# ScalarE in program order in the dense attentions, and a regrouped layer-3 FFN, in an eight-block transformer kernel

## The chip, the core and the metric

The kernel runs on one NeuronCore of a Trainium2 chip, in one launch. The core has five engines, each with an instruction queue of its own that it works off in order: TensorE (PE; its weight loads, PEld, are listed apart), VectorE (DVE), ScalarE (ACT), GpSimd (POOL), and SyncE (SP), which issues most DMAs. They wait for one another by semaphores. The metric is the device time of the launch in microseconds (us), the median of several runs.

## What is computed

The input x has 4 sequences of 512 rows of 128 channels, all float32. Four layers follow, each a "macaron": half of an FFN, an attention, half of the same FFN again.

```python
x = x + 0.5 * ffn_l(layernorm(x))
x = x + attn_l(layernorm(x))
x = x + 0.5 * ffn_l(layernorm(x))
```

The blocks that the change touches:

- **Layer-1 FFN**: a causal attention with 16 heads of 8 channels over all 512 rows, then a layer norm with weights (ln1), a gate over 8 experts of which two count, the experts' 128x128 products summed by the gates, and a second layer norm with weights (ln2).
- **Layer-3 attention**: 16 heads of 8, not causal, rotary queries and keys, biases on q, k, v and on the output (bo).
- **Layer-3 FFN**: two inner layers, each:

```python
h = shift_token(x)                       # half of the channels one row later
q, k, v = split(h @ wqkv)                # 8 heads of 64
o = local_attention(rotary(l2norm(q) * qs), rotary(l2norm(k) * ks), v)   # window 64
x = x + o @ wo
h = shift_token(x)
h = (h - mean(h)) / sqrt(var(h) + 1e-5) * lg + lb
a, g = split(h @ w1 + b1)                # 2 x 341
x = x + (a * gelu(g)) @ w2 + b2
```

The other blocks (layer 0, the layer-1 and layer-2 attentions, the routed layer-2 FFN) are left as they are.

## The kernel before

Rows lie on the 128 partitions as 16 tiles; TB = 4 tiles make a sequence b. Python loops write out all instructions. A scheduler then places them on the engines by estimated times and dependencies, except those handed to keep_in_program_order: these keep their order on their engine. Before the change all matmuls and transposes of these blocks are so held (mm_in_order, transpose_in_order), and the layer-3 FFN's ACT instructions (act, act_copy). DVE and POOL are free, and so is ACT in the dense attentions.

**Dense attention** (dense_attention, used by the layer-1 FFN with a causal mask and by the layer-3 attention without one). A unit is (sequence b, j) with four heads; it has four steps n of two half steps each. In a half step, PE writes scores pk_at, writes products pq_at for the maxima five steps ahead (LEAD), ACT turns pk_at into PT by Exp (L778), the maxima nm are taken on DVE (L743 unmasked, L748 masked), and PE multiplies PT of the step before with the values (po_at). The banks in PSUM: one double bank for pk_at, two for pq_at, one for po_at, one ("m") for all else. Work for the next sequence hangs at places relative to its first step: prepare gives pairs (place, function); half steps are tenths .5. marked_keys (L676) makes four copies of the keys with head channels masked, two on ACT (L683), two on DVE (L685). After each half step, tick runs parts of "chains": lists of (gap, function), each part due gap ticks after the one before. The experts of the layer-1 FFN (l1_experts) are such a chain: statistics of y, affine(1) (y scaled on ACT at L223 by scaled_by_act, then two products with the weights on POOL, or on DVE for the last sequence), turn, gates, choice, eight products, statistics, affine(2), residual. The root in the statistics is some ten small POOL steps (L184 to L194).

**Layer-3 FFN** (l3_ffn). A unit is (inner layer l, sequence b), eight in all, with four steps each; a step n runs stages for several tiles at once: project(n), exponentials(n-4), to_features(n-2), weights(n-3), turn_weights(n-5), with_values(n-6), at places 0 to 5. Around them stand the unit's parts from a list of (function, step after the unit's first, place); a part runs just before the stage of its place. PSUM has three double banks "d" (p_qk, pt_qk, ps3, pt3 and pag take turns in them) and two single "m".

```python
parts = [
    (attended, 10, 2), (mean, 10, 4), (variance, 11, 0), (normed, 11, 4), (lambda u: hidden(u, 0), 12, 2),
    (lambda u: hidden(u, 1), 12, 3), (lambda u: hidden(u, 2), 12, 5), (close_unit, 13, 2),
    (lambda u: leave(units[u][1]) if units[u][0] else None, 13, 5),
]
```

attended multiplies with wo (pz), adds into z = yT (L1690) and makes h by a shift, half on ACT, half on DVE (L1548). mean subtracts the mean (L1699) and squares (sq). variance sums the squares (pvar), copies them to rs (L1711), takes the root on POOL (rs L194), and spreads it over a diagonal dg (L1714, DVE). normed multiplies by ones (pb) and applies the norm in two DVE steps (L1724, L1725). hidden(u, c) makes one of three chunks of the gated product: pag on PE, Gelu on ACT into ge, hh on DVE (L1738). Gelu and Exp are in different ACT tables, so each group of gelus has two table loads.

Of the kernel before, what the change touches and what calls it, by code (L numbers as in the profile page):

```python
# [103 lines left out]
def tile_macaron(ctx, tc, x_in, const_in, vec_in, w0_in, ws_in, ws3_in, w2f_in, w3_in, out):  # L104
# [104 lines left out]
    def scaled(dst, src, b, stats):  # L209

        mv, r = stats
        for t in range(b * TB, b * TB + TB):
            i = t - b * TB
            nc.vector.tensor_scalar(dst[:, t, :], src[:, t, :], mv[:, i, 0:1], r[:, i : i + 1], ALU.subtract, ALU.mult)  # L214

    def scaled_by_act(dst, src, b, stats):

        mv, r = stats
        m = keep.tile([P, TB], F32, tag="ln_m", name="ln_m", bufs=3)
        nc.vector.scalar_tensor_tensor(m, mv[:, :, 0], -1.0, r, ALU.mult, ALU.mult)  # L220
        for i in range(TB):
            t = b * TB + i
            nc.scalar.activation(dst[:, t, :], src[:, t, :], AF.Identity, scale=r[:, i : i + 1], bias=m[:, i : i + 1])  # L223

    def normalize(dst, src, b, pinned=False):
        scaled(dst, src, b, statistics(src, b, None, pinned))
# [1 line left out]
    def turn(b):  # L228

        pt = bank("m", "pt_y")  # L230
        for t in range(TB):
            transpose_in_order(pt[:, ts(t, P)], y[:, b * TB + t, :])
        nc.scalar.copy(yT[:, b, :], pt)  # L233

# [441 lines left out]
    def marked_keys(sb, src, bias):  # L676


        km = sb.tile([P, 4, S], F32, tag="km", name="km", bufs=2)
        for j in range(4):  # L680
            mj, bj = kmask[:, j : j + 1], bias[:, j : j + 1]
            if j % 2:
                nc.scalar.activation(km[:, j, :], src, AF.Identity, scale=mj, bias=bj)  # L683
# [28 lines left out]
    def dense_attention(sb, prepare, finish, wo, masked, tiles=None):  # L712

        vhs, nms = tiles or attention_tiles(sb)
        seqs, units = {}, [(b, j) for b in range(B) for j in range(4)]
        n_steps = TB * len(units)
        qxs, PTs, pos, later = {}, {}, {}, {}
# [55 lines left out]
        def weights(step, half, pk):  # L775
            q0 = step % TB * P if masked else 0
            PT = sb.tile([P, 2, S], F32, tag="PT", name="PT", bufs=4)
            nc.scalar.activation(PT[:, :, q0:], pk[:, :, q0:], AF.Exp, scale=SC8)  # L778
# [36 lines left out]
        def output(b):  # L815
            pt = bank("m", "pt_ao")
            for t in range(TB):
                transpose_in_order(pt[:, ts(t, P)], seqs[b]["ao"][:, t, :])
            aoT = sb.tile([P, S], F32, tag="oT", name="aoT")
            nc.scalar.copy(aoT, pt)  # L820
            seqs[b]["aoT"] = aoT

        def project(b):
# [21 lines left out]
        for n in range(-LEAD, n_steps + 5):  # L845
            for half in range(2):
                pk = scores(n, half) if 0 <= n < n_steps else None
                if n + LEAD < n_steps:
                    maxima(n + LEAD, 1 - half)
                if pk is not None:  # L850
                    weights(n, half, pk)
                if 1 <= n <= n_steps:
                    with_values(n - 1, half)
                    if half and n % TB == 0:
                        u = n // TB - 1
                        oTs[u] = sb.tile([P, S], F32, tag="oT", name="oT")
                        nc.scalar.copy(oTs[u], pos.pop(u))
# [4 lines left out]
        assert not later, later  # L862


    def l1_ffn(tag, xb, l1_tiles):

        with pool(tag) as sb, banks(tag + "ps", **MIX):
# [4 lines left out]
            def prepare(b, vh, seq):  # L872
                def norm():
                    seq["ready"] = take(b)
                    if not seq["ready"]:
                        seq["stats"] = statistics(x, b)

                def scale():
                    if not seq["ready"]:
                        scaled(y, x, b, seq.pop("stats"))  # L880

                def features():
                    if not seq["ready"]:
# [12 lines left out]

                def queries():
                    pq = bank("m", "pq1")
                    mm_in_order(pq, WS(ws, "1f_wq"), seq["in"])
                    seq["q"] = sb.tile([P, S], F32, tag="qT", name="qT", bufs=2)  # L900
                    nc.scalar.activation(seq["q"], pq, AF.Identity, bias=bq)

                def keys():
                    pk = bank("m", "pk1")
                    mm_in_order(pk, WS(ws, "1f_wk"), seq["in"])
                    kT = sb.tile([P, S], F32, tag="kT", name="kT")
                    nc.scalar.copy(kT, pk)
# [14 lines left out]
    def l1_experts(sb, b):  # L922
# [15 lines left out]
        def gates():  # L938
# [8 lines left out]
            nc.scalar.activation(g, g, AF.Exp)  # L947

        def choice():
            g, r = st["g"], st["r"]  # L950
# [10 lines left out]
        def turn_gates():  # L961
# [4 lines left out]
            nc.scalar.copy(st["gT"], pt[:8, :])  # L966

        def biases():
            pb = bank("m", "pb")
# [41 lines left out]

        spare = chain(b)
        spare(2, statistics_of_y, False)
        spare(2, lambda: affine(1), False)
        spare(4, lambda: turn(b))
        alone = b == B - 1 and routed
        if alone:
# [14 lines left out]
            else:  # L1032
                spare(2, lambda t=t: both(t))
        spare(1, statistics_of_y, False)
        spare(2, lambda: affine(2), False)
        spare(2, residual, False)
        leave_normed(b, spare, 2)

# [441 lines left out]
    def l3_attn():  # L1480
        with pool("l3a") as sb:
            with banks("l3apa", **MIX):

                def prepare(b, vh, seq):
# [6 lines left out]
                    def second(n):  # L1491
# [2 lines left out]
                        t2 = sb.tile([P, S], F32, tag="t2", name="t2", bufs=2)  # L1494
                        nc.vector.scalar_tensor_tensor(t2, p2, WS3(ws3, f"3a_b{n}s"), ST, ALU.add, ALU.mult)
                        nc.gpsimd.tensor_add(seq[n], seq[n], t2)
                        if n == "k":
                            seq["k"] = marked_keys(sb, seq["k"], kmax)

                    return (  # L1500
                        (-14, lambda: begin_sequence(b)), (-13.5, lambda: first("k")), (-12, lambda: second("k")),
                        (-10.5, lambda: first("q")), (-9, lambda: second("q")),
                        (-7.5 if b else -4, lambda: values(vh, b, WS3(ws3, "3a_v"), VEC(vec, "3a_bv"))),
                    )

                def finish(b, pr):
                    xb = x[:, ts(b, TB), :]
                    nc.vector.tensor_add(xb, pr, xb)
                    nc.gpsimd.tensor_add(xb, xb, rows(VEC(vec, "3a_bo"), TB))
                    leave_normed(b, chain(b), 3)  # L1510

                dense_attention(sb, prepare, finish, WS3(ws3, "3a_o"), False)
# [9 lines left out]
    def l3_ffn(w3, tag, first):  # L1522
        with pool(tag) as sb, banks(tag + "ps", d=3, m=2):
# [180 lines left out]
            def variance(u):  # L1704
# [5 lines left out]
                rs = sb.tile([P, TB], F32, tag="rs", name="rs", bufs=2)  # L1710
                nc.vector.tensor_copy(rs, pv[:, : 2 * TB].rearrange("p (t i) -> p t i", i=2)[:, :, 0])  # L1711
                inverse_root(sb, rs, rs, "ir4", ALU.add, 1e-5, nc.gpsimd)
                dg = tmp("dg")
                nc.vector.scalar_tensor_tensor(  # L1714
                    dg.rearrange("p (t n) -> p t n", n=P), rows(ident, TB), float(D), bcast(rs, P), ALU.mult, ALU.mult
# [3 lines left out]
            def normed(u):  # L1719
# [1 line left out]
                h2 = u_state[u]["h2"]  # L1721
                pb = bank("m", "pb3")
                mm_in_order(pb, onesm, u_state[u].pop("dg"))
                nc.vector.tensor_mul(h2, h2, pb)  # L1724
                nc.vector.tensor_scalar(h2, h2, W(l, "lg"), W(l, "lb"), ALU.mult, ALU.add)  # L1725

            def hidden(u, c):
                l, b = units[u]
# [35 lines left out]
            if first:  # L1764
                for l in range(2):
                    tab = W(l, "tab").rearrange("p (t n) -> p t n", t=TB)
                    nc.vector.tensor_mul(tab, tab, rows(VEC(vec, f"3f_s{l}"), TB))

            parts = [
                (attended, 10, 2), (mean, 10, 4), (variance, 11, 0), (normed, 11, 4), (lambda u: hidden(u, 0), 12, 2),  # L1770
                (lambda u: hidden(u, 1), 12, 3), (lambda u: hidden(u, 2), 12, 5), (close_unit, 13, 2),
                (lambda u: leave(units[u][1]) if units[u][0] else None, 13, 5),
            ]
            later = {}
            for u in range(len(units)):
# [192 lines left out]
```

## Time and profile before

| | us |
|---|---|
| median of 3 runs | 2975.86 (2975.21 to 2979.55) |
| the profiled execution | 2971.15 |
| its span, first to last instruction | 2969.5 |
| busy: PE, DVE, ACT, POOL | 2266.3, 1828.9, 1242.9, 908.0 |
| layer-1 FFNs, from the first to the last Exp | some 450 to 760 and 940 to 1255 |
| layer-3 FFNs, first to last projection | 1681 to 2028 and 2531 to 2872 |
| layer-3 attention, first to last Exp | 2164 to 2515 |

Page and trace come from one execution, with times from the span's start. A busy share is an average over stages with different limits, so the views by window count most. In the list of waits, a line names the engine and line that waited, what released it, the total, how often, and the longest. The chain that ended last follows the end back through whatever released each step:

```profile
PE 49%; DVE 24%; ACT 11%; POOL 10%; issue 6%; DMA 1%; DVEq 0%; POOLq 0%; ACTq 0%; SPq 0%
```

### The profile page before, as it was taken

To read this page: it belongs to the slowest core of one execution; us is meant where nothing else is said; L and a number is where in the kernel's file an instruction comes from. 1 tells how busy PE (TensorE), PEld (TensorE's weight loads), DVE (VectorE), ACT (ScalarE), POOL (GpSimd) and SP (SyncE) were. 2 spreads that over 40 slices of the span, in tenths; PEclk is the share of its full clock that TensorE was granted. 3 is DMA by queue.
4 is the path that set the end of the run, shared out by engine and by line. 5 is a ranking of instruction groups with operands and counts; after the bars stand their busy time and mean duration, and the time that the engine had idled before them with its cause. 6 is when DMAs were issued, how large, how long until landed. Compare 5 with 4: busy or idle time off the path is not lost.

```text
span 2969.5 us, 46865 instructions
## 1 busy us (share of the span) xinstructions
PE 2266.3 (76%) x17534; PEld 1171.2 (39%) x17534; DVE 1828.9 (62%) x4796; ACT 1242.9 (42%) x2682; POOL 908.0 (31%) x1668
## 2 busy tenths in 40 slices
PE   4377439888678898849668578888688898688987
PEld 2145113333333333338358355555322222455553
DVE  4656476666576576554654587776455554787773
ACT  3054304433332433314323276666134344476663
POOL 1022012232122222212412486664100000777651
PEclk8588759999787999969768799998789999899998
DMA  3042010000000000017007210000000000110000
GB/s 132 0 154 76 0 58 1 1 1 1 1 1 1 1 1 4 5 57 257 15 16 263 72 26 19 21 19 9 0 1 1 1 1 1 26 24 18 23 19 11
DMA packets 33771, 99.12 MB, mean 33 GB/s; under 512 B 6184, under 2 KB 12072, under 8 KB 33032
## 3 DMA queue, kind: packets, MB, share of 16 engines
q1 hardware_dynamic: 30616, 88.03, 9.1%
q0 software_dynamic: 2496, 5.12, 0.8%
q8 instruction: 138, 2.26, 0.3%
q10 hardware_dynamic: 432, 2.98, 0.3%
q14 instruction: 89, 0.73, 0.1%
HBM read 66.88 MB, written 14.55 MB: 27 GB/s over the span
## 4 chain that ended last, share of the span: by engine, by line
PE 49%; DVE 24%; ACT 11%; POOL 10%; issue 6%; DMA 1%; DVEq 0%; POOLq 0%; ACTq 0%; SPq 0%
PE pk_at L164 10%; PE po_at L164 6%; ACT PT L778 4%; PE pa L164 3%; PE po L164 3%; PE pe L164 3%; PE pag L164 2%; PE pv L164 2%; DVE y L987 2%; PE pz L164 2%; PE pt L161 2%; PE pg L164 2%; POOL t L1591 2%; ACT s L1536 2%; DVE order L357 1%
## 5 line engine op out<-in xcount | busy, mean ns | idle before, releaser
L778 ACT ACTIVATE PT<-pk_at 128x1024 f32<-128x1024 f32 (+3 forms) x384 | 311.1, 810 | 535.0 <-PE pq_at L164 461.8
L164 PE MATMUL pk_at<-qx,km 32*128 32x512 f32 (+3 forms) x1536 | 370.6, 559 | 87.4 <-ACT PT L778 85.0
L164 PE MATMUL po_at<-PT,vh 128*32 128x512 f32 (+3 forms) x1536 | 335.8, 519 | 0.3 <-ACT PT L778 0.2
L748 DVE CUSTOM_DVE_ANT_0 s<-pq_at,cst 128x384 f32<-128x384 f32 (+3 forms) x512 | 248.5, 485 | 97.2 <-PE pq_at L164 85.4
L1536 ACT ACTIVATE s<-s,nm,rn 128x128 f32<-128x128 f32 x512 | 245.6, 485 | 14.2 <-DVE nm L1642 14.0
L781 POOL TENSOR_SCALAR_AFFINE_SELECT PT<-PT 128x256 f32<-128x256 f32 x256 | 106.9, 419 | 439.1 <-ACT PT L778 439.0
L164 PEld LDWEIGHTS pk_at<-qx,km 32*128 32x128 f32 x1536 | 121.1, 192 | 298.4 <-ACT PT L778 240.1
L164 PE MATMUL pq_at<-km,qT 32*128 32x384 f32 (+3 forms) x1024 | 223.9, 526 | 13.5 <-DVE nm L748 7.7
L743 DVE TENSOR_REDUCE nm<-pq_at 128x2 f32<-128x1024 f32 x128 | 156.4, 1225 | 115.1 <-PE pq_at L164 115.0
L1591 POOL TENSOR_TENSOR t<-t,t 128x1024 f32<-128x1024 f32 x64 | 151.3, 2364 | 152.7 <-DVE t L1587 149.9
L161 PE MATMUL pt_y<-ident,y 128*128 128x128 f32 x224 | 54.3, 369 | 166.2 <-DVE y L214 94.5
L164 PE MATMUL pq_at<-km,t 32*128 32x512 f32 x512 | 152.0, 700 | 5.0 <-DVE nm L743 2.8
L233 ACT COPY yT<-pt_y 128x512 f32<-128x512 f32 x56 | 32.8, 586 | 272.8 <-PE pt_y L161 272.8
L164 PE MATMUL p_qk<-w,hT 128*128 128x512 f32 x256 | 136.4, 658 | 13.2 <-DVE t L1587 9.1
L164 PEld LDWEIGHTS po_at<-PT,vh 128*32 128x32 f32 x1536 | 55.9, 109 | 218.1 <-issue 153.8
L1654 POOL TENSOR_TENSOR s<-s,sm 128x1024 f32<-128x1024 f32 x64 | 121.8, 1904 | 50.9 <-DVE sm L1653 46.0
L1536 ACT ACTIVATE sq<-p_qk 128x1024 f32<-128x1024 f32 x64 | 65.6, 1025 | 136.0 <-PE p_qk L164 90.1
L161 PE MATMUL pt<-ident,s 128*128 128x128 f32 x640 | 96.2, 299 | 33.9 <-POOL s L1654 14.3
L1584 DVE TENSOR_TENSOR t<-p_qk,w 128x1024 f32<-128x1024 f32 x64 | 78.2, 1221 | 60.9 <-ACT sq L1536 60.5
L161 PEld LDWEIGHTS pt_y<-ident,y 128*128 128x128 f32 x224 | 33.5, 168 | 199.3 <-issue 119.7
L164 PE MATMUL pag<-h,w 128*128 128x512 f32 (+1 forms) x192 | 101.7, 662 | 11.3 <-DVE h L1725 10.1
L161 PEld LDWEIGHTS pt<-ident,s 128*128 128x128 f32 x640 | 80.1, 154 | 69.3 <-issue 43.5
(421 smaller groups left out, 5149.3 us busy)
## 6 DMA issues: line engine op xcount, KB each, us to landing
w<-in_w2f_dram SPq DMA_DIRECT2D x46, 836.0 KB, 6.7
vb<-v SPq DMA_DIRECT2D x112, 128.0 KB, 2.2
skew<-qe SPq DMA_DIRECT2D x16, 512.0 KB, 3.0
rel<-skew SPq DMA_DIRECT2D x64, 128.0 KB, 3.4
w<-in_w_dram SPq DMA_DIRECT2D x1, 4147.0 KB, 12.6
w<-in_w_dram SPq DMA_DIRECT2D x1, 3200.0 KB
od<-o SPq DMA_DIRECT2D x46, 64.0 KB, 5.0
yd<-y SPq DMA_DIRECT2D x8, 256.0 KB, 2.3
```

The lines of the kernel that those rows point to most:

```text
L161: return nc.tensor.transpose(dst, src, ident[: src.shape[0], : src.shape[0]])
L164: tc.keep_in_program_order(nc.tensor.matmul(dst, lhsT=lhsT, rhs=rhs, start=start, stop=stop))
L233: nc.scalar.copy(yT[:, b, :], pt)
L743: nc.vector.tensor_reduce(to, pq.rearrange("p (i n) -> p i n", i=2), AX.X, ALU.max)
L748: nc.vector.tensor_tensor_reduce(s[:, :nk], pq[:, i * 512 : i * 512 + nk], causal[:, S - nk :], 1.0, -BIG, ALU.add, ALU.max, nm[:, qt, at ...
L778: nc.scalar.activation(PT[:, :, q0:], pk[:, :, q0:], AF.Exp, scale=SC8)
L781: nc.gpsimd.affine_select(d, d, pattern=[[0, 2], [1, P]], base=0, channel_multiplier=-1, compare_op=ALU.is_ge, fill=0.0)
L987: nc.vector.scalar_tensor_tensor(yt, pe[e // 4][:, ts(e % 4, D)], st["g"][:, t, e : e + 1], yt, ALU.mult, ALU.add)
L1536: tc.keep_in_program_order(nc.scalar.activation(*args, **kw))
L1584: nc.vector.tensor_mul(by_head(t1), by_head(p3), over(tab[:, 0]))
L1591: nc.gpsimd.tensor_add(t1, t1, t2)
L1654: nc.gpsimd.tensor_mul(s, s, bcast(sm, P))
```

## The change

1. A switch, ordered["act"], is on while a dense attention is written out; by_order then holds ACT's instructions in program order: PT, oT, aoT, qT, kT, the two ACT keys, yT, g, gT and the norm's y.
2. scaled_by_act makes m = -mean * r by two POOL steps instead of one DVE step. affine(1) and affine(2) of the experts come four ticks after the statistics instead of two.
3. Layer-3 attention: the keys are marked by a function of its own at place -11, not at the end of second("k") at -12; the output bias bo is added to x there, not after the projection.
4. Layer-3 FFN: exponentials and to_features change places, so that qT is copied before the exponentials; spread (dg) is a part of its own, half a step after variance; normed is one DVE step with lg, while lb goes through w1 into b1, once at the start (pn); the parts get other places, with hidden 0 at the end of one step and hidden 1 and 2 at the start of the next.

```diff
+    ordered = {"act": False}
+    def by_order(i):
+        if ordered["act"]:
+            tc.keep_in_program_order(i)
     def scaled_by_act(dst, src, b, stats):
-        nc.vector.scalar_tensor_tensor(m, mv[:, :, 0], -1.0, r, ALU.mult, ALU.mult)
+        nc.gpsimd.tensor_mul(m, mv[:, :, 0], r)
+        nc.gpsimd.tensor_scalar_mul(m, m, -1.0)
...
-            nc.scalar.activation(dst[:, t, :], src[:, t, :], AF.Identity, scale=r[:, i : i + 1], bias=m[:, i : i + 1])
+            by_order(nc.scalar.activation(dst[:, t, :], src[:, t, :], AF.Identity, scale=r[:, i : i + 1], bias=m[:, i : i + 1]))
...
-            nc.scalar.activation(PT[:, :, q0:], pk[:, :, q0:], AF.Exp, scale=SC8)
+            by_order(nc.scalar.activation(PT[:, :, q0:], pk[:, :, q0:], AF.Exp, scale=SC8))
...
-        spare(2, lambda: affine(1), False)
+        spare(4, lambda: affine(1), False)
...
-        spare(2, lambda: affine(2), False)
+        spare(4, lambda: affine(2), False)
...
                         nc.gpsimd.tensor_add(seq[n], seq[n], t2)
-                        if n == "k":
-                            seq["k"] = marked_keys(sb, seq["k"], kmax)
+                    def mark():
+                        seq["k"] = marked_keys(sb, seq["k"], kmax)
+                        xb = x[:, ts(b, TB), :]
+                        nc.gpsimd.tensor_add(xb, xb, rows(VEC(vec, "3a_bo"), TB))
...
-                        (-10.5, lambda: first("q")), (-9, lambda: second("q")),
+                        (-11, mark), (-10.5, lambda: first("q")), (-9, lambda: second("q")),
...
                     nc.vector.tensor_add(xb, pr, xb)
-                    nc.gpsimd.tensor_add(xb, xb, rows(VEC(vec, "3a_bo"), TB))
...
                 inverse_root(sb, rs, rs, "ir4", ALU.add, 1e-5, nc.gpsimd)
+                u_state[u]["rs"] = rs
+            def spread(u):
+                rs = u_state[u].pop("rs")
                 dg = tmp("dg")
...
                 mm_in_order(pb, onesm, u_state[u].pop("dg"))
-                nc.vector.tensor_mul(h2, h2, pb)
-                nc.vector.tensor_scalar(h2, h2, W(l, "lg"), W(l, "lb"), ALU.mult, ALU.add)
+                nc.vector.scalar_tensor_tensor(h2, h2, W(l, "lg"), pb, ALU.mult, ALU.mult)
...
+                    pn = bank("m", "pn")
+                    w1, a = W(l, "w1"), W3.at[f"lg{l}"][0]
+                    for half, name in ((0, "b1a"), (1, "b1g")):
+                        for c, (at, n) in enumerate(HCH):
+                            i = 2 * (3 * half + c)
+                            mm_in_order(pn[:n, i : i + 2], w1[:, half * HID + at : half * HID + at + n], w3[:, a : a + 2])
+                            to = W(l, name)[:n, c : c + 1]
+                            nc.vector.tensor_add(to, to, pn[:n, i + 1 : i + 2])
...
-                (attended, 10, 2), (mean, 10, 4), (variance, 11, 0), (normed, 11, 4), (lambda u: hidden(u, 0), 12, 2),
-                (lambda u: hidden(u, 1), 12, 3), (lambda u: hidden(u, 2), 12, 5), (close_unit, 13, 2),
-                (lambda u: leave(units[u][1]) if units[u][0] else None, 13, 5),
+                (attended, 10, 2), (mean, 10, 4), (variance, 11, 0), (spread, 11, 4), (normed, 12, 0),
+                (lambda u: hidden(u, 0), 12, 5), (lambda u: hidden(u, 1), 13, 0), (lambda u: hidden(u, 2), 13, 0),
+                (close_unit, 13, 4), (lambda u: leave(units[u][1]) if units[u][0] else None, 14, 0),
...
-                    (project, 0), (exponentials, 4), (to_features, 2), (weights, 3), (turn_weights, 5), (with_values, 6)
+                    (project, 0), (to_features, 2), (exponentials, 4), (weights, 3), (turn_weights, 5), (with_values, 6)
```

More of the change, by code (lines that the diff above doesn't have):

```diff
@@ L232, in turn @@
             transpose_in_order(pt[:, ts(t, P)], y[:, b * TB + t, :])
-        nc.scalar.copy(yT[:, b, :], pt)
+        by_order(nc.scalar.copy(yT[:, b, :], pt))
     clock, chains = [0], []
@@ L682, in marked_keys @@
             if j % 2:
-                nc.scalar.activation(km[:, j, :], src, AF.Identity, scale=mj, bias=bj)
+                by_order(nc.scalar.activation(km[:, j, :], src, AF.Identity, scale=mj, bias=bj))
             else:
@@ L716, in dense_attention @@
         vhs, nms = tiles or attention_tiles(sb)
+        ordered["act"] = True
         seqs, units = {}, [(b, j) for b in range(B) for j in range(4)]
@@ L819, in output @@
             aoT = sb.tile([P, S], F32, tag="oT", name="aoT")
-            nc.scalar.copy(aoT, pt)
+            by_order(nc.scalar.copy(aoT, pt))
             seqs[b]["aoT"] = aoT
@@ L856, in dense_attention @@
                         oTs[u] = sb.tile([P, S], F32, tag="oT", name="oT")
-                        nc.scalar.copy(oTs[u], pos.pop(u))
+                        by_order(nc.scalar.copy(oTs[u], pos.pop(u)))
                 fs = later.pop((n, half), ())
@@ L862, in dense_attention @@
         assert not later, later
+        ordered["act"] = False
     def l1_ffn(tag, xb, l1_tiles):
@@ L900, in queries @@
                     seq["q"] = sb.tile([P, S], F32, tag="qT", name="qT", bufs=2)
-                    nc.scalar.activation(seq["q"], pq, AF.Identity, bias=bq)
+                    by_order(nc.scalar.activation(seq["q"], pq, AF.Identity, bias=bq))
                 def keys():
@@ L906, in keys @@
                     kT = sb.tile([P, S], F32, tag="kT", name="kT")
-                    nc.scalar.copy(kT, pk)
+                    by_order(nc.scalar.copy(kT, pk))
                     seq["k"] = marked_keys(sb, kT, bkm)
@@ L946, in gates @@
             nc.vector.tensor_sub(g, g, bcast(r, 8))
-            nc.scalar.activation(g, g, AF.Exp)
+            by_order(nc.scalar.activation(g, g, AF.Exp))
         def choice():
@@ L965, in turn_gates @@
             st["gT"] = sb.tile([8, S], F32, tag="gT", name="gT")
-            nc.scalar.copy(st["gT"], pt[:8, :])
+            by_order(nc.scalar.copy(st["gT"], pt[:8, :]))
         def biases():
```

## The prediction

> **What bounds the kernel now.** I read the page first. TensorE (PE) is busy 76% of the 2969.5 us span and has 49% of the chain that ended last; VectorE (DVE) has 24%. No engine is full, so the next view is the busy time by stage: the first layer-1 FFN, the layer-3 attention, and the first layer-3 FFN up to its last projection. Columns: window and length, busy us of PE, weight load, DVE, ACT (ScalarE), POOL (GpSimd), granted clock, DMA share, GB/s.
>
> ```profile
> 450.00:760.00 310.00, 275.30 (x1804) 105.71 (x1804) 195.75 (x777) 119.14 (x189) 83.43 (x193) 0.93 0.00 1
> 2165.00:2520.00 355.00, 317.40 (x1712) 85.01 (x1712) 190.35 (x248) 146.67 (x157) 11.39 (x9) 0.97 0.00 1
> 1722.00:2027.00 305.00, 265.07 (x2380) 160.16 (x2381) 233.99 (x341) 206.17 (x552) 214.30 (x419) 0.96 0.09 20
> ```
>
> PE is close to full in all three and idles 35 to 40 us in each. Who makes it wait? The waits of these windows, in the same order (waiting engine and line, what it waits for: us, times, longest):
>
> ```profile
> ACT y L223 <- DVE ln_m L220: 12.5, 3, 5.0
> ...
> DVE ln_m L220 <- POOL ln_r L194: 8.5, 3, 3.4
> ...
> ACT km L683 <- POOL t L1496: 15.6, 3, 6.2
> ...
> DVE dg L1714 <- POOL rs L194: 22.1, 5, 4.5
> ...
> DVE hh L1738 <- ACT ge L1536: 14.8, 10, 1.9
> ...
> PE ps L164 <- DVE hh L1738: 13.2, 5, 2.6
> ```
>
> Each is one instruction at the head of an engine's queue. While ACT holds y or km, the exponentials PT (L778) behind it cannot free the score bank pk_at, which has one buffer, and PE stops. The timeline shows it in the layer-3 attention (start, length, engine; idle time before it in brackets); windows around two such gaps show the granted clock, the number after POOL's:
>
> ```profile
> 2282.42 1.52 ACT L683 ACTIVATE km<-t,cst 128x512 f32<-128x512 f32 x2 [6.24 <-POOL t L1496]
> ...
> 2284.90 1.22 PE L164 MATMUL pk_at<-qx,km 32*128 32x512 f32 x2 [5.75 <-ACT PT L778]
> ...
> 2190.30:2192.80 2.50, 0.00 (x0) 0.00 (x0) 2.13 (x3) 2.43 (x4) 0.04 (x1) 1.00 0.00 0
> 2193.00:2196.40 3.40, 3.40 (x12) 0.47 (x12) 1.23 (x1) 1.29 (x2) 0.00 (x0) 0.50 0.02 5
> ...
> 2284.90:2288.60 3.70, 3.70 (x12) 0.70 (x12) 1.23 (x1) 1.45 (x2) 0.00 (x0) 0.51 0.00 0
> ```
>
> PE does nothing for 5.75 us, and then its pairs take 1.22 us where they took 0.70: the gap costs twice.
>
> **Layer-1 FFNs: ScalarE in program order, ln_m on GpSimd.** PE idles 3.27, 4.50 and 4.76 us before pk_at in the first and 3.24, 4.50 and 3.17 in the second, 23.4 us together. Each time ACT holds y (L223), which waits for ln_m on DVE, which waits for POOL's root (ln_r). In the order that the changed program has on the engines, y stands three to five half steps later (behind the second 256-wide PT instead of the first 1024 or 384), and ln_m is on POOL directly behind its root. A unit of eight half steps took 14.5 to 17 us where nothing was added, so three are 6 us, more than the longest wait of 5.0. Both waits go, DVE's too. What is late next: y x4 (4x0.41), kT (0.58) and two km (1.5) now stand in a row on ACT, 3.7 us where the half step covers some 2.2: about 1.5 us of PE idle remains at four of the six places, 6 us. Clock: half speed followed the gaps for 3.4, 6.8 and 13.7 us in the first FFN, at most 12 us lost; the rows behind have other waits too, so I take 3.5 for each FFN. Sum: -(23.4 - 6) - 7 = **-24**; ends -10 and -40.
>
> Here a rule speaks against the edit: the Trainium skill (GPSIMD Engine Reference, 4.1 Engine selection) sends elementwise work to VectorE, since GpSimd takes about twice as long with two inputs. Row: ln_m takes 0.16 us on DVE, POOL's 128x4 product 0.20 and its scalar step 0.19. Two POOL steps for one on DVE cost 0.23 us more by the row, 0.48 if 0.16 is doubled for both: 16 times, 3.7 or 7.7 us of POOL. POOL is 27% busy here and covers either; only the last chain of the second FFN (some 1254 to 1300 us) lies bare, **+1**. I take the row; the edit's worth is the wait, not the duration. The experts' chains get four ticks longer and spill further into the layer-1 attention, where PE, DVE and ACT wait by turns: 0 to +4, taken as **+2**.
>
> **Layer-3 attention.** The keys' mark moves one step later, and x+bo (1.26 us on POOL) leaves the end of a sequence. ACT's 15.6 us of waiting for POOL's t go; PE idled 2.59, 5.75 and 5.75 us for them. But DVE isn't held to program order: in the changed order its two km still stand directly behind t (L1495) and ahead of nm. So DVE waits as before: t, POOL 1.27, km 1.0, then nm. The product bank pq_at has two buffers, so PE runs one half step on and stops at the next: nm ends at about 2284.3, pq_at is wanted at 2281.9, 2.4 us idle, at two places. Gain: 2x(5.75-2.4) + 2.6 = 9.3, and slow clock. There rule and row differ: the Trainium skill (TensorE: Matmul & The Clock Gate, Part 1) halves the clock after an idle window of about 3.4 us, which clears gaps of 2.4; in the rows above 2.59 us of idle was followed by 3.4 us at 0.50. By the rule all slow time goes (17 us, 8.5 saved), by the row only that at the first place (1.7). I stay near the row, 3.2: **-12.5**; ends -5 and -20. The four x+bo stand in the FFN before, ahead of POOL's root in its last steps: 1.3 on a chain there once or twice, **+2**.
>
> **Layer-3 FFNs.** DVE issues L1584 once a step. In one unit of four steps the starts lie 15.0 (attended, mean), 7.6, 17.2 (the gated products) and 9.7 us apart; by the starts of sq the mean of ten full units is 49.1. The third of them in the timeline:
>
> ```profile
> 1890.32 1.28 ACT L1536 ACT_TABLE_LOAD   x1
> ...
> 1892.20 0.58 ACT L1539 COPY qT<-pt_qk 128x512 f32<-128x512 f32 x1
> ...
> 1893.14 1.99 PE L164 MATMUL ps<-kT,qT 64*64 64x128 f32 x32 [2.64 <-DVE hh L1738]
> ```
>
> qT stands behind the exponentials, a table load and a gelu, and PE waits. DVE's work in a plain step, by its rows: 1.22 + 2x0.68 + 1.21 + kT 0.67 + s 1.22 + 0.20 + nm 1.21 + 0.29 + oT 0.68 = 8.05. The new steps, from start to start of L1584:
> - attended: z stands behind kT (4.5) and ends at 5.1 (pz is done at 4.0: p_qk 1.92, pv 0.86, pt_qk 0.87, pz 3.45, less 3.1 from p_qk's start to L1584's); ACT's h ends at 5.8. The exponentials now stand behind h, where they ran beside pz before: 3.9 us, to 9.7; sm 9.9, POOL's s to 11.8, root 2.9 to 14.7, dg 0.7: **15.4**. For dg still stands directly behind rs on DVE: spreading the variance in the source moves nothing there.
> - next: 8.05 and the one normed step, 0.75 (price of L1738, for 0.68 and 0.54): **8.8**.
> - gated: s frees pag's bank at 5.7, two products 3.4, p_qk 1.95, sq 1.0: **12.1**. qT is ahead, and nothing on PE waits for a gelu.
> - close: 8.05 + z 0.74 + hT 0.98: **9.8**.
>
> Together 46.1 for 49.1; ten units give -30. A half unit before each drain gives -1.5 more; in the drains nothing runs beside h, +2.5, less 0.5 for normed and 0.5 for the gelus: these cancel. **-30**; ends -61 and +5. The 2-column products and twelve DVE sums for b1 run once before the first projection, where PE waits for gathers: 12x0.16, nothing on the path, 2 us if that cover is gone. SP's order stays as it was, no DMA is moved.
>
> **Sum** against the profiled execution, 2971.15 us (span 2969.5): -24 + 1 + 2 - 12.5 + 2 - 30 = -61.5, so 2909.7. The runs' median, 2975.86, lies 4.7 higher: **2914**.
>
> **Rivals.**
> 1. The stalls go wholly (0.17). For: ACT and POOL have 30% of the FFN window free, and half clocks go with the gaps. Against: dg's place. A unit at the larger of PE's and DVE's work, step by step (11.1, 9.0, 9.4, 12.8; PE's plain step 6.75), is some 43: -61. Layer 1 -36, attention -19, +2: 2862.
> 2. A new wait eats the FFN part (0.17): h holds the exponentials and dg holds DVE, a unit stays at 49. Layer 1 -16, attention -10, +5: 2955.
> 3. Slower (0.05): the same h. ACT idles some 3.8 us in each attended step; I let that pass once. If the late s also holds the transposes pt of the next step, and these the exponentials behind them, the unit pays it twice more: 46.1 + 7.6 = 53.7, +46 for ten units, -31.5 elsewhere: 2990. It decides from a unit of 52.3 us. Against: s is ready at 11.8, those transposes come some 5 us later.
> 4. Gains and losses cancel within 0.2%, about what a measurement of this kernel can tell (0.03).
>
> **How the numbers follow.** The forecast has 0.58, its own range 2890 to 2935. Faster: 0.58 + 0.17 + 0.17 = 0.92; same 0.03; slower 0.05. The range for 8 times in 10 reaches from rival 1 to rival 2, 2860 to 2956; what lies beyond is rival 3 and the halves of 1 and 2.
>
> **What would show it.** ACT's waits for ln_m and for POOL's t gone, PE's idle time before pk_at under 2 us in layer 1; in the attention PE waiting for nm instead; in the FFN dg still waiting for POOL, the attended step at 15 and the gated one at 12 instead of 17. Wrong if dg's wait is gone, if a unit is off 46 by over 2, or if instructions of the experts stop ACT at new places in layer 1.

## The result, and the profile after

| | before | after |
|---|---|---|
| median (lowest to highest), us | 2975.53 (2971.83 to 2979.55, 4 runs) | 2935.83 (2931.72 to 2941.97, 4 runs) |
| span of the profiled execution | 2969.5 | 2934.6 |
| layer-1 FFN, first and second, first to last Exp | 310.2, 307.2 | 299.9, 311.7 |
| from there to the routed layer's product pi | 74.2 | 77.7 |
| layer-3 FFN, first and second, first to last projection | 344.7, 340.1 | 338.6, 333.5 |
| layer-3 attention, first to last Exp | 350.2 | 335.8 |

The stages are measured from start to start, in one profile each. The ratio is 0.9868 (95% interval 0.9846 to 0.9890): 39 us faster, where 61.5 were forecast. The changed kernel's busy time in the three stages that the prediction began with (columns as there: window and length, busy us of PE, weight load, VectorE, ScalarE, GpSimd, then granted clock, DMA share, GB/s):

```profile
450.00:757.00 307.00, 274.92 (x1838) 105.37 (x1836) 199.12 (x779) 120.37 (x192) 87.45 (x206) 0.95 0.00 1
2157.00:2495.00 338.00, 312.67 (x1704) 83.89 (x1704) 187.71 (x246) 146.34 (x156) 7.61 (x6) 0.99 0.00 1
1722.00:2020.00 298.00, 263.67 (x2380) 161.33 (x2381) 226.45 (x336) 207.87 (x553) 214.14 (x421) 0.95 0.09 21
```

PE still idles some 32 to 34 us in the first and third window; only the attention came down, to 25. The waits of the same windows say what stands there now (waiting engine, what it waits for: us, times, longest):

```profile
PE pk_at L164 <- ACT PT L787: 18.7, 24, 1.7
PE pt_y L161 <- DVE vh L715: 2.6, 1, 2.6
...
DVE km L693 <- POOL t L1506: 3.8, 3, 1.4
PE pq_at L164 <- DVE nm L752: 2.0, 2, 1.0
...
DVE dg L1731 <- POOL rs L194: 17.3, 5, 3.8
DVE hh L1754 <- ACT ge L1548: 10.8, 10, 1.2
```

ScalarE's waits for ln_m and for GpSimd's t are gone, as forecast, and so are PE's pauses of 3 to 5 us before pk_at in layer 1 (longest now 1.7; a new one of 2.6 stands before pt_y). In the attention VectorE's keys wait in their place, and PE waits 1.0 us for nm at two places. dg waits for GpSimd as before. The chain that ended last has hardly changed its make-up:

```profile
PE 51%; DVE 22%; ACT 10%; POOL 9%; issue 6%; DMA 2%; SPq 0%; POOLq 0%; DVEq 0%; ACTq 0%
```

### The profile page after: what moved, and what is told of

Same layout as the page of the kernel before. It is cut to its first block, busy times and chain, and to the rows that moved or that the text cites. A ratio compares the mean times of both kernels' runs of the same rounds, so it can differ in the third digit from the quotient of the medians.

```text
span 2934.6 us, 46900 instructions
## 1 busy us (share of the span) xinstructions
PE 2274.4 (78%) x17558; PEld 1179.6 (40%) x17558; DVE 1808.6 (62%) x4776; ACT 1246.5 (42%) x2682; POOL 913.9 (31%) x1700
## 4 chain that ended last, share of the span: by engine, by line
PE 51%; DVE 22%; ACT 10%; POOL 9%; issue 6%; DMA 2%; SPq 0%; POOLq 0%; DVEq 0%; ACTq 0%
PE pk_at L164 10%; PE po_at L164 6%; ACT PT L787 4%; PE pa L164 3%; PE pag L164 3%; PE po L164 3%; PE pe L164 3%; PE p_qk L164 2%; POOL t L1603 2%; PE pg L164 2%; DVE t L1599 2%; PE pv L164 2%; DVE t L1596 2%; DVE y L997 2%; PE pq_at L164 2%
## 5 line engine op out<-in xcount | busy, mean ns | idle before, releaser
L164 PE MATMUL pq_at<-km,qT 32*128 32x384 f32 (+3 forms) x1024 | 225.9, 530 | 14.1 <-DVE nm L757 7.7
L164 PE MATMUL p_qk<-w,hT 128*128 128x512 f32 x256 | 144.0, 691 | 10.8 <-DVE t L1599 9.0
L1666 POOL TENSOR_TENSOR s<-s,sm 128x1024 f32<-128x1024 f32 x64 | 121.5, 1898 | 49.1 <-DVE sm L1665 41.0
L1596 DVE TENSOR_TENSOR t<-p_qk,w 128x1024 f32<-128x1024 f32 x64 | 78.3, 1223 | 71.4 <-ACT sq L1548 71.1
L1290 DVE SCALAR_TENSOR_TENSOR hT<-pa,w,sg 128x128 f32<-128x128 f32 x184 | 51.8, 345 | 85.1 <-ACT sg L1289 64.0
```

The costliest lines, as they stand in the source:

```text
L164: tc.keep_in_program_order(nc.tensor.matmul(dst, lhsT=lhsT, rhs=rhs, start=start, stop=stop))
L1596: nc.vector.tensor_mul(by_head(t1), by_head(p3), over(tab[:, 0]))
L1666: nc.gpsimd.tensor_mul(s, s, bcast(sm, P))
```

## The experiments

All ratios are against the kernel before, from runs beside it on the same chip. The stage lengths, in us, come from one profile each, taken as in the table above; they separate the stages, which the whole time does not. The unit is the mean of five full units of the second layer-3 FFN, split at VectorE's first product of each step.

| kernel | ratio (95% interval) | layer-1 FFNs | to routed | layer-3 FFNs | l3 attention | attended, next, gated, close = unit |
|---|---|---|---|---|---|---|
| before | 1 | 310.2, 307.2 | 74.2 | 344.7, 340.1 | 350.2 | 15.0, 8.3, 16.1, 9.7 = 49.1 |
| p1 layer 1 alone | 0.9995 (0.9984 to 1.0006) | 305.4, 313.7 | 77.7 | 341.3, 343.0 | 349.9 | |
| p2 attention alone | 0.9936 (0.9918 to 0.9953) | 310.2, 307.2 | 74.2 | 346.7, 337.5 | 338.3 | |
| p3 layer-3 FFN alone | 0.9928 (0.9911 to 0.9945) | 310.2, 307.2 | 74.2 | 338.4, 333.6 | 349.5 | 15.1, 9.3, 13.8, 9.5 = 47.6 |
| p4 all again | 0.9874 (0.9859 to 0.9890) | 300.2, 308.2 | 77.6 | 338.3, 333.1 | 335.7 | 15.2, 8.9, 13.8, 9.5 = 47.3 |
| e1 | 0.9903 (0.9886 to 0.9921) | 300.4, 308.2 | 77.6 | 340.5, 333.6 | 335.8 | 14.1, 10.3, 13.8, 9.5 = 47.7 |
| e2 | 0.9942 (0.9929 to 0.9954) | 305.4, 313.7 | 77.7 | 344.5, 338.4 | 335.4 | 15.1, 10.4, 13.8, 9.5 = 48.8 |
| e3 | 0.9870 (0.9855 to 0.9885) | 305.4, 307.7 | 77.7 | 331.8, 325.0 | 338.0 | 12.6, 10.3, 13.7, 9.5 = 46.2 |
| e4 | 0.9963 (0.9949 to 0.9976) | 300.4, 308.2 | 77.6 | 349.4, 343.1 | 335.4 | 15.0, 10.7, 14.3, 9.8 = 49.7 |
| b1 | 0.9785 (0.9762 to 0.9808) | 305.4, 313.7 | 77.7 | 324.1, 320.9 | 335.4 | 12.6, 9.4, 13.8, 9.5 = 45.3 |
| b2 | 0.9772 (0.9752 to 0.9793) | 302.5, 303.3 | 74.2 | 326.6, 320.6 | 335.4 | 12.6, 9.4, 13.8, 9.5 = 45.3 |
| b3 | 0.9784 (0.9760 to 0.9809) | 306.7, 307.2 | 74.2 | 325.2, 321.0 | 335.5 | 12.6, 9.7, 13.8, 9.5 = 45.5 |
| e6 | 0.9911 (0.9891 to 0.9930) | 303.7, 318.6 | 77.5 | 338.0, 333.6 | 335.4 | |

### Each part alone

p1 takes only the switch for the masked attention, ln_m and the gaps of four; p2 only the switch for the unmasked one, the mark at -11 and bo; p3 only the layer-3 FFN; p4 is the whole change once more.

> Only the layer-1 part: ScalarE in program order in the masked attention, ln_m on GpSimd, affine gaps of four ticks. The prediction's own sum for this part: -24 + 1 + 2 = -21 us, both layer-1 FFNs shorter by some 12 each. Rival A (the trace of the full change): the first FFN gains 10, the second loses 4 and the routed layers behind it lose 5, because the instructions that stood at good places on ScalarE are now held at fixed ones: about 0 to -2 us in all. Rival B (clock luck): both FFNs gain some 10, and the second FFN's loss in the one profile was a half-clock stretch that another run does not show: -12 to -20 us.

> Only the layer-3 attention part: ScalarE in program order there, keys marked one step later, x+bo with them. Prediction: -12.5 + 2 = -10.5 us, PE waiting 2.4 us for nm at two places. Rival (stalls go wholly): -19 us. From the trace of the full change: the stage is 14.4 us shorter, with nm waits of 1.0 us at two places, so -14 to -16 us.

> Only the layer-3 FFN part. Prediction: -30 us, unit 46.1 (attended 15.4, next 8.8, gated 12.1, close 9.8). Rival 2 of the prediction: 0 us, unit 49. From the trace of the full change: -6.1 and -6.6 in the two projections' stretches and -4.6 in the last drain, -17 us, with a gated step of 13.8.

> The whole change once more, for a second profile. If the parts add up, its gain is the sum of the three parts within 4 us. If the second layer-1 FFN's loss of 4.4 us (first to last Exp 311.7 us, half-clock 54.5 us) belongs to the program, this profile shows 311 to 313 again; if it is clock luck, it shows 305 or less with 10 to 25 us less half-clock time.

Layer 1 brought -1.5 us (+1.8 to -4.8), the attention -19.0 (-14.0 to -24.4), the FFN -21.4 (-16.4 to -26.5): together -42, and p4 gave -37.5 (-32.7 to -41.9). So the parts add up within their intervals, and they are not the forecast's parts: -21, -10.5, -30. Which of p2's three edits brings the attention's gain was not tried apart.

For layer 1 neither rival is the whole truth. The same instructions in the same order on PE, VectorE, ScalarE and GpSimd up to layer 3 (the whole change, p1, p4, e1 to e4, b1) took 299.9 to 305.4 us in the first FFN and 307.7 to 313.7 in the second; of the layer 1 of before, three profiles (before, p2, p3) agree within 0.1 us.

What scatters is the time at half clock, summed from each trace's record of the granted clock: in the first FFN 31.6 us of it went with 300.2 (p4) and 41.8 with 305.4 (p1), in the second 52.2 with 308.2 and 64.5 with 313.7, about half of the difference each time, while PE's idle time stays at 63 to 65 us for both FFNs. In all fourteen profiles the clock keeps each of its two levels for a whole multiple of 3.41 us, so where a pause falls against these steps can differ between executions; that this is why the same order scatters is not shown.

The last unit of the second FFN in p4, by window and then in the timeline of PE (start, length, engine, line; idle before it in brackets):

```profile
1219.00:1223.00 4.00, 2.32 (x16) 0.72 (x14) 3.02 (x16) 2.46 (x4) 0.53 (x2) 0.94 0.00 0
1223.00:1227.00 4.00, 4.00 (x10) 1.06 (x12) 0.00 (x0) 1.10 (x2) 0.69 (x2) 0.50 0.00 0
...
1235.00:1239.00 4.00, 4.00 (x18) 1.27 (x15) 0.00 (x0) 0.98 (x2) 0.81 (x2) 0.50 0.00 0
```

```profile
1220.55 1.13 PE L164 MATMUL pk_at<-qx,km 32*128 32x512 f32 x4 [0.84 <-ACT PT L787]
...
1222.87 1.65 PE L164 MATMUL pk_at<-qx,km 32*128 32x384 f32 x4 [0.84 <-ACT PT L787]
1224.44 1.92 PE L164 MATMUL po_at<-PT,vh 128*32 128x512 f32 x4
```

Two pauses of 0.84 us, 1.5 us apart, and the clock is 0.50 for at least the next 16 us, with PE busy all the while. In before the same pauses stand 16.8 us apart and the clock stays at 1.00. But it does not take the pair: in the profile of the result half clock is there behind the first pause, for the four products after it already take 2.08 us instead of 1.13, before the second:

```profile
1221.30 1.13 PE L164 MATMUL pk_at<-qx,km 32*128 32x512 f32 x4
...
1223.61 2.08 PE L164 MATMUL pk_at<-qx,km 32*128 32x512 f32 x4 [0.84 <-ACT PT L787]
...
1226.87 1.65 PE L164 MATMUL pk_at<-qx,km 32*128 32x384 f32 x4 [0.61 <-ACT PT L787]
```

What divides the profiles is the gaps of four, not ScalarE's order. A stretch of 18.2 to 21.8 us at half clock ends the second FFN in all nine profiles with gaps of four, e6 with its free order among them, and in none of the five with gaps of two (before, p2, p3, b2, b3). At half clock the second FFN spends 51.7 to 69.4 us in the nine and 37.3 to 44.2 in the five. By these profiles, then, the longer gaps cost the second FFN time at half clock that the held order alone does not (303.3 and 307.2 us in b2 and b3, 307.7 to 313.7 with both).

### What removes ScalarE's waits in layer 1

```diff
-        ordered["act"] = True
+        ordered["act"] = not masked
```

> The whole change, with ScalarE free again in the masked attention (layer 1); ln_m on GpSimd, gaps of four ticks and all of layer 3 stay. Theory (the later place and ln_m beside its root take the waits away, the held order does not): PE's waits of 3 us and more before pk_at stay away, and the first FFN is within 3 us of 300 to 305. Rival (the held order is what removes them): y stands earlier, waits of 3 to 5 us return at up to three places, and the FFN is at 308 to 310 again.

Held order against free order, the waits of the first FFN in e6:

```profile
ACT y L231 <- POOL ln_m L228: 12.3, 3, 4.7
...
PE pk_at L164 <- ACT PT L787: 26.8, 25, 4.8
```

The wait is back at its old size (12.5 before), though ln_m stands on GpSimd beside its root and the gap is four: y stands further forward in ScalarE's queue again. PE pauses 3.67, 2.04 and 4.81 us before pk_at for ScalarE, and 3.65 us once for VectorE's qx. The FFNs' lengths did not follow cleanly, 303.7 and 318.6, so of the two signs that were named only the waits decide: the held order removes them. PE's idle time (length less busy) is 77.7 us for both FFNs here, 64.7 in p4, 71.1 before. By the ratios e6 is 11 us slower than p4, give or take 7.

### The gaps of four, and ln_m's engine

b2 is b1 (below) with two edits taken back, b3 is b2 with a third:

```diff
-        spare(4, lambda: affine(1), False)
+        spare(2, lambda: affine(1), False)
...
-        spare(4, lambda: affine(2), False)
+        spare(2, lambda: affine(2), False)
```

> b1_dg_between with the experts' affine steps two ticks after their statistics again, as before the change; ScalarE stays in program order. Theory (the four ticks push the last sequences' experts out of the attention): the stretch from the second FFN's last Exp to the routed layer's first product goes from 77.6 back to some 74.2 us, and PE's long waits before pk_at come back in part (y one half step earlier, waiting for ln_m): layer 1 within +-5 us of b1. Rival (the longer stretch is ln_m's place on GpSimd): 77 us again.

The 3.5 us between the second FFN and the routed layer belong to the gaps: 74.2 with two, 77.6 with four. In p4 eight groups of the experts' products (pe) start after the last Exp, in before and in b2 seven. PE's waits came back in part (2.31 us at two places of each FFN), yet the FFNs took 302.5 and 303.3 us: they were at half clock for 28.2 and 39.3 us, in b1 for 41.8 and 64.6. In the whole time b2 is 3.9 us below b1, give or take 9, so a gain is not shown there.

```diff
-        nc.gpsimd.tensor_mul(m, mv[:, :, 0], r)
-        nc.gpsimd.tensor_scalar_mul(m, m, -1.0)
+        nc.vector.scalar_tensor_tensor(m, mv[:, :, 0], -1.0, r, ALU.mult, ALU.mult)
```

> b2_and_gaps_two with ln_m as one VectorE step again, as before the change (ScalarE stays in program order). By the rule on engine selection, and by the rows alone, GpSimd's two steps cost more than VectorE's one: 0 to -4 us against b2. By the prediction's argument ('the edit's worth is the wait, not the duration') VectorE holds ln_m up to 3.4 us for GpSimd's root again, with what is queued behind it: PE's waits before pk_at in the two FFNs grow by up to 8.5 us each, +4 to +12 us against b2. If VectorE's queue has slack at those places: within 3 us.

2907.44 us against 2905.82: no difference that shows (by the ratios 3.6 us, give or take 10), in spite of VectorE waiting 8.5 and 9.9 us for ln_r again. ScalarE's y waits 3.0 us for it in the first FFN, where it waited 12.5 before. The engine of ln_m is worth too little to be seen, though the 4 us and more of the second expectation are not excluded. The profile's FFNs are 4 us longer each, but the stretch between them is 5.6 us shorter.

### Copies ahead

```diff
-                    (project, 0), (to_features, 2), (exponentials, 4), (weights, 3), (turn_weights, 5), (with_values, 6)
+                    (project, 0), (exponentials, 4), (to_features, 2), (weights, 3), (turn_weights, 5), (with_values, 6)
```

> The whole change, with the exponentials again ahead of to_features, so that qT is copied behind them as before; all other parts stay. If the FFN's gain comes from qT's place ('copies ahead'): +12 to +20 us against the whole change, with PE waiting for qT in every step. If it comes from the gated products' places and from normed's one step: 0 to +6 us. The attended step alone should get shorter, since h does not hold the exponentials then.

It cost more than the upper end: 11.1 us in the first FFN, 10.0 in the second, and 26 by the ratios. The unit is 49.7, none of the gain left: it hangs on qT's place, and the other edits of the FFN bring nothing without it. The attended step did not get shorter (15.0), which already spoke against h as its cause.

### What sets the attended step

e1 (spread goes to place 1):

```diff
-                nc.vector.tensor_mul(by_head(t1), by_head(p3), over(tab[:, 0]))
+                tc.keep_in_program_order(nc.vector.tensor_mul(by_head(t1), by_head(p3), over(tab[:, 0])))
...
-                nc.vector.tensor_copy(
+                tc.keep_in_program_order(nc.vector.tensor_copy(
...
-                nc.vector.scalar_tensor_tensor(
+                tc.keep_in_program_order(nc.vector.scalar_tensor_tensor(
...
-                (attended, 10, 2), (mean, 10, 4), (variance, 11, 0), (spread, 11, 4), (normed, 12, 0),
+                (attended, 10, 2), (mean, 10, 4), (variance, 11, 0), (spread, 11, 1), (normed, 12, 0),
```

> The whole change, with dg held on VectorE behind the three products and the sum of the step's new tile (in place of directly behind rs). Theory of the prediction: dg's wait for GpSimd's root holds those products by about 2.3 us in each attended step (they could start at 1914.9, behind p_qk, and start at 1917.1), so the attended step goes from 15.2 to about 13 us and eight units give -14 to -18 us against the whole change. Rival: VectorE is not what is late there; PE waits next for GpSimd's product s, whose place in GpSimd's queue does not change, and the step stays at 15: 0 to -4 us, or +4 if pb now waits for dg.

e2 changes `(attended, 10, 2)` to `(attended, 10, 3)` and nothing else; e3 is both.

> The whole change, with attended one place later, so that on ScalarE the shift h stands behind the step's eight exponentials and not ahead of them; PE's order is the same. Theory (the prediction's 'h holds the exponentials'): they start 3.5 us earlier in the attended step, s and the square behind them come 1.8 to 3.5 us earlier, h itself at most 0.5 us later: attended step from 15.2 to 12 to 13.4, eight units -14 to -25 us against the whole change. Rival: the exponentials run into h's way, the mean waits for them, and the chain mean, square, root is as long as before: within 3 us of the whole change.

> Both edits together. If the two are one chain (h, exponentials, square, root, dg, products), the second brings what the first leaves: -20 to -28 us against the whole change, attended step about 12, where PE's own work in it (some 11 us) ends the gain. If each takes the same stall, no more than the better of the two.

By the ratios none of the three beat the whole change: against p4, e1 was 8.6 us slower (give or take 7), e2 20 (give or take 6), and e3 level (1.2 faster, give or take 6), where -20 to -28 were expected. e3's FFNs are 6.5 and 8.1 us shorter than p4's, but in that profile its layer-1 FFNs are 4.7 us longer, with the same order, and its attention 2.3. Of e2's 20 us, 11.5 stand in the layer-3 FFNs and 10.7 in those of layer 1.

e1: the attended step fell, to 14.1, and the next rose by as much. e2: the exponentials ended 4 us earlier, and the step stayed at 15.1. Its timeline shows why; GpSimd, VectorE and PE, one after the other:

```profile
1821.23 2.37 POOL L1603 TENSOR_TENSOR t<-t,t 128x1024 f32<-128x1024 f32 x1 [0.90 <-DVE t L1599]
...
1826.74 1.04 POOL L1604 TENSOR_TENSOR t<-t,rn 128x512 f32<-128x512 f32 x1
...
1828.23 1.90 POOL L1666 TENSOR_TENSOR s<-s,sm 128x1024 f32<-128x1024 f32 x1 [0.29 <-POOL h L1559]
...
1833.04 0.20 POOL L194 TENSOR_TENSOR rs<-ir 128x4 f32<-128x4 f32 x1
...
1833.27 0.69 DVE L1731 SCALAR_TENSOR_TENSOR dg<-ident,rs 128x512 f32<-128x512 f32 x1 [4.75 <-POOL rs L194]
...
1836.44 1.62 PE L161 MATMUL pt<-ident,s 128*128 128x128 f32 x8 [3.53 <-ACT s L1548]
```

GpSimd works with hardly a pause (0.3 us) from 1821.23 to 1833.24: sum, root of rn, product, s, root of rs. With sm ready at 1824.1, s still starts at 1828.23, where its queue comes to it; in the whole change s starts at the same distance from the step's start (9.8 us, here 9.6) with sm just in time. Two chains of equal length ended there, ScalarE's and GpSimd's queue, and e2 shortened one. It lost in the next step: PE's pause is now one of 3.53 us, where the whole change has two in a full unit (in p4 1.3 us up to 1911.99, 2.1 up to 1919.70), and half clock follows it (pt 1.62 us, not 1.06). Here the trace agrees with the Trainium skill (TensorE: Matmul & The Clock Gate, Part 1), by which an idle window of about 3.4 us halves the clock: in the first FFN five pauses of 3.3 to 3.6 us before pt are each followed by half clock.

e3 takes dg out of that chain and h too: 12.6, with PE busy 12.0 of it. Each edit alone gave time back in the next step, and so do both: that step took 8.9 in p4 and takes 10.3, so 1.4 of the 2.6 us go again. It is not one chain but two that end together, and it takes both edits to free the attended step. In the next one VectorE is full, by the window of that step in e3, and dg is slow:

```profile
1820.97:1831.30 10.33, 7.85 (x89) 4.87 (x88) 10.33 (x12) 6.82 (x21) 8.31 (x22) 1.00 0.05 13
```

```profile
1824.43 2.02 DVE L1731 SCALAR_TENSOR_TENSOR dg<-ident,rs 128x512 f32<-128x512 f32 x1
...
1823.54 2.37 POOL L1603 TENSOR_TENSOR t<-t,t 128x1024 f32<-128x1024 f32 x1 [0.64 <-DVE t L1599]
```

dg took 2.02 us for 0.69 and ended 0.54 after GpSimd's sum. So b1 puts dg between the two products of L1599, before that sum starts (and lets go of two other VectorE steps that e1 and e3 held):

```diff
+            due = []
             def project(step):
...
+                held = tc.keep_in_program_order if due else lambda i: i
                 for half in range(2):
                     a, z = ts(half, 32), ts(1 - half, 32)
-                    nc.vector.tensor_mul(by_head(t2[:, :, a]), by_head(p3[:, :, z]), over(tab[:, 1, :, a]))
+                    held(nc.vector.tensor_mul(by_head(t2[:, :, a]), by_head(p3[:, :, z]), over(tab[:, 1, :, a])))
+                    if due:
+                        spread(due.pop())
...
-                nc.vector.scalar_tensor_tensor(
+                tc.keep_in_program_order(nc.vector.scalar_tensor_tensor(
...
-                (attended, 10, 2), (mean, 10, 4), (variance, 11, 0), (spread, 11, 4), (normed, 12, 0),
+                (attended, 10, 3), (mean, 10, 4), (variance, 11, 0), (due.append, 11, 0), (lambda u: spread(due.pop()) if due else None, 11, 4), (normed, 12, 0),
```

> As e3_both (h behind the exponentials, dg behind the next tile's products), but dg stands between the two 0.6 us products of L1599 in place of behind L1601. In e1 and e3 dg took 2.03 us, not 0.69, and ended 0.55 us after GpSimd's 128x1024 sum (L1603) each time, and the step was VectorE's alone (10.33 of 10.33 us busy). Theory (VectorE's dg and GpSimd's large sum exclude each other): between the products dg is over before that sum starts, takes 0.7 us, and the step goes from 10.33 to some 8.7 to 9.0 us: eight units -10 to -13 us against e3. Rival (dg is slow for another reason, or PE's p_qk sets the step): it stays above 10 us and the time within 3 us of e3.

VectorE's and GpSimd's timeline in b1:

```profile
1832.92 0.69 DVE L1736 SCALAR_TENSOR_TENSOR dg<-ident,rs 128x512 f32<-128x512 f32 x1 [0.21 <-POOL rs L194]
...
1834.36 2.38 POOL L1608 TENSOR_TENSOR t<-t,t 128x1024 f32<-128x1024 f32 x1 [1.32 <-DVE t L1602]
```

dg takes 0.69 again. The step is 9.4, not the 8.7 to 9.0 expected, but well under 10.3, and the FFNs are 7.7 and 4.1 us shorter than in e3. By the ratios b1 is 25 us below e3, give or take 8; only the FFNs' 11.8 are what the theory names. With b2's gaps the kernel runs in 2905.82 us (2902.18 to 2909.65), faster than both kernels of this study.

## Why the prediction was right, and where not

The time fell on the side that was named and within the range for 8 times in 10, 0.8 us outside the forecast's own 2890 to 2935; the sum was 22 us too large. By the whole times layer 1 brought 19.5 us less than its part, the layer-3 FFNs 8.6 less and the attention 8.5 more. That the one covered some of the others is luck. By its own steps:

- **Layer-1 FFNs, -24 (with +1 and +2): this step failed.** Its mechanism held in part: y stands later, both waits are gone, e6 shows that the order does it, and PE's pauses before pk_at are under 2 us. Two terms did not. "-(23.4 - 6)": PE's idle time fell by 6.4 us, not 17.4 (71.1 to 64.7 in p4). The long pauses fell from 23.4 to 10.5, with new ones among them before pt_y (2.6 and 2.9, for vh) and po_at (1.6); the rest is many small ones. "-7" for the clock: PE's busy time changed by -2.6 (p4), +0.5 (the profile of the result) and +9.7 (p1), for the second FFN's time at half clock rose from 37.4 us to 51.7 and more, with the gaps of four (above). And "+1" for the last chain was 3.5, which is the gaps' and not ln_m's. Together -1.5 (p1) for -21.
- **Layer-3 attention, -10.5: right mechanism, too small.** km on VectorE behind t, PE waiting for nm at two places: so it is, but the wait is 1.0 us and not 2.4. Pauses: 2x(5.75 - 1.0) + 2.6 = 12.1 for 9.3; PE's busy time 3.4 less, for 3.2. That the 3.2 came so close is luck: it assumed that most of the 17 us at half clock stay, and in the profile of the result all are gone (1.00 from 2165.3 us to the stage's end); but in each of the two stretches of 6.8 us PE had been busy for only 3.7. The stage is 14.4 us shorter. Of the +2 for x+bo nothing can be said: the FFN before it is 2.0 us longer in p2, and 3.4 shorter in p1, where its code is that of before.
- **Layer-3 FFNs, -30: right mechanism, too large.** Forecast 15.4, 8.8, 12.1, 9.8 = 46.1; measured 15.2, 8.9, 13.8, 9.5 = 47.4 in the second FFN. (Of the unit of before that the prediction read, the next and the gated step are 8.1 and 16.7 in the trace, not 7.6 and 17.2; its sum hardly changes.) The one wrong term is the gated step's "s frees pag's bank at 5.7, two products 3.4". The timeline of that step in the changed kernel:

```profile
1887.16 1.21 DVE L1649 TENSOR_TENSOR s<-ps,cst 128x1024 f32<-128x1024 f32 x1
...
1887.30 1.99 PE L164 MATMUL pag<-h,w 128*128 128x512 f32 x4 [0.38 <-DVE kT L1628]
...
1889.21 0.34 PE L164 MATMUL po<-PT,vb 128*64 128x64 f32 x4
...
1890.29 3.70 PE L164 MATMUL pag<-h,w 128*128 128x512 f32 x8
...
1893.83 1.89 PE L164 MATMUL p_qk<-w,hT 128*128 128x512 f32 x4
```

  The bank is free at 1888.37, 5.3 us after the step's start at 1883.10, but PE comes to these products 1.9 us later. It does not wait meanwhile: from 1887.30 it is busy with hidden 0's product and then with po, 32 products in 1.1 us, which stand ahead of them in its order and for which the sum has no term. Ten units of 1.7 are 17 us of the 30; the two stretches of projections are 12.8 us shorter in p3, and the whole part brought -21.4.
- **"Spreading the variance moves nothing there":** dg did stay behind rs, and attended came out at 15.2. But the reason was only half of it: the exponentials behind h were one of two equal chains, the other GpSimd's queue (e2).
- **Rivals.** Rival 1 (no stall left) names -19 for the attention, which p2 gave by the whole time, but two waits of 1.0 us are left and the stage shows 14.4. Rival 2 (a unit stays at 49) did not come about, though both waits that it names are there: the step came free only when both were moved (e3). Rival 3 did not occur: the unit stayed at 47.4, far from 52.3. Rival 4 holds for layer 1 by itself: gains and losses cancelled.
- **The rules weighed.** That GpSimd is dearer than VectorE made no difference that shows (b3). The clock rule was weighed against a row with half clock after 2.59 us; e2 agrees with the rule, layer 1 with neither: there one pause of 0.84 us preceded the longest slow stretch, and in before pauses of the same length did not.

What stays open: why the clock stays at half for 16 us and more in the last unit of the second layer-1 FFN while PE is busy, and what in the gaps of four brings this about. That it goes with them is read from one profile of each kernel; the whole times do not show it (b2 against b1).

## What to carry over

A stall of an engine that is taken away is worth what PE's idle time loses, not what the stall lasted: the next wait or work in PE's own order (here pt_y's wait for vh, and po) takes the rest, and PE's busy time can grow by time at half clock. So walk PE's queue instruction by instruction past the place. Before moving work out of a late chain, look whether a second engine's queue ends at the same moment, and change both together. And measure each part of a change alone, by stage: here a part worth nothing, -1.5 us, carried a third of the forecast.

## What was not expected of the hardware

- A VectorE step with two inputs in SBUF and a GpSimd sum did not run beside each other: dg took 2.02 us and ended 0.54 after the sum's end in e3, 0.69 us away from it in b1. The Trainium skill (SBUF — State Buffer, Who interferes with whom) says that a VectorE step with two inputs in SBUF contends with a GpSimd step that reads SBUF, and calls the ports that they share an exclusive lock; these runs agree, but for some 0.15 us, by which 0.54 is less than the 0.69 of dg alone.
- Half clock lasted 16 us and more with PE busy 4.00 of every 4.00 us (p4), and in the profile of the result it began behind a single pause of 0.84 us.
- In all fourteen profiles every stretch at one clock is a whole multiple of 3.41 us long (3.41, 6.83 and 10.24 us among them).
- Programs with the same order in a layer differed by 5.5 us (first FFN) and 6.0 us (second) from profile to profile, where those of the kernel before repeated within 0.1 us.
